# Keys of edge lists on GpSimd, and a norm's scalings split between ScalarE and VectorE, in a four-layer graph network

## The chip, the cores and the metric

The kernel runs on one core of a Trainium2 chip. The metric is the device time of the whole program in microseconds (us), shorter being better. Its inputs lie in HBM, and so does its output. Engines are named as the profile names them: PE is TensorE, DVE is VectorE, ACT is ScalarE, POOL is GpSimd, and SP is SyncE, whose queue carries most DMAs.

## The reference

The graph has 2048 nodes with 64 features each, in 8 batches. All batches share one symmetric adjacency matrix of int32, 2048 by 2048, with about 9 entries in a row, the diagonal among them. Four layers follow one another, each as `x = layernorm(x + layer(x, adj))`:

```
layer 0: h = layernorm(W(x*nw + nb + x)); softmax over the neighbours of leaky_relu(s1[i] + s2[j]); att @ h + h; elu
layer 1: f = softplus(x*w0 + b0); softmax over the neighbours, for each feature by itself; sum of the weights times f
layer 2: relu(x @ W_self + b_self + mean of the neighbours' x @ W_neigh + b_neigh); a layer norm of its own
layer 3: 4 heads of attention over neighbours with scores h.h; joined, leaky_relu, W_o; a fifth such attention; leaky_relu; layer norm
```

Layer 2 thus ends in two norms in a row: its own, with gain and shift, and then that of the sum `x + layer(x)`.

## The kernel before

Nodes are taken in 16 tiles of 128, one node to a partition. The tensor `X` holds the features of all nodes in SBUF through all layers, in fp32. The program is a row of stages, and each stage has pools of its own. "bufs=2" below means that a name has two buffers in turn, so that the third instance waits until the first has been read.

**The adjacency stage** (lines 296 to 383) makes two things out of the matrix: for tiles 0 to 8 a transposed copy of it for PE (`ET`, line 335), and for every tile a list of its edges. The loop goes over the 16 tiles, and a scheduler orders the instructions of every engine by their dependencies and priorities. For a tile:

- `at` (128 x 2048, int32, bufs=3) is loaded on SP's queue; `X` of the tile is loaded on ACT's queue.
- `key` (f16, bufs=2, line 327) is the number of the column, from 1, where there is an edge, and 0 elsewhere. One DVE instruction makes it from `at` and `node_no`.
- `on` (line 329) is the sign of it, by ACT, which adds up the degree `deg` at the same time. PE turns `on` over for the first nine tiles.
- Eight Max8 instructions on 256 columns each (line 338) give the largest keys of each segment in `tops`. Three rounds of Max8 and MatchReplace (lines 343 and 345) pick the 24 largest of those in order: the neighbours, `nbr`.
- `junk` (lines 347 and 349) counts the own edge and the list. A product on PE (line 354) gives every node its offset in the list of its group, `offs`; `ends` is the offset plus the degree.
- `nbrs` (line 359) holds four copies of a node's list, each kept in only one of the four groups of 32 nodes.
- `first_of` and `SelT` (lines 362 and 363) say which of the 384 places of a list belong to which node. PE multiplies `nbrs` by them (line 369) into `pl`; `at_`, `hit` and `src` (lines 373 to 380) turn `pl` into the row numbers that the gathers use later. `Sel` (line 371) is `SelT` turned over.
- After every second tile `node_products` makes layer 0's products and norm of two tiles; ACT squares at line 279, DVE adds up at 280, and `S1` at line 293 is its last instruction.

**Layer 0 and layer 1** follow. POOL issues layer 0's gathers of rows from `htab` in HBM (line 186), by `src`. Lines 539 to 548 belong to layer 1: there POOL casts `R` and subtracts (lines 544 and 548) beside DVE's `rest` (line 546).

**Layer 2** first makes products of every tile (lines 743 to 761, POOL's cast and subtraction at 754 and 760). In its main phase the order of PE, ACT, DVE and POOL is written out by hand, one step of PE after another: matrix products for tiles 0 to 8 (line 899), with the products over gathered rows for tiles 15 down to 9 (line 879) spread between them. `finish` (lines 844 and 845) makes a finished tile's sum with `S`, its ReLU, and takes its statistics. Tiles are put together in groups of the sizes `[1, 2, 3, 4, 3, 1, 1, 1]`; a full group becomes a `chain`, a Python generator of which `advance` takes a step or two after each step of PE:

- `newton` makes the factors of the first norm, by some twelve small DVE instructions.
- The first norm scales `S` into `z` in PSUM, one instruction to a batch (line 788 on ACT; in the last groups, where `shared` is true, every second one on DVE, line 786). `z` is multiplied by the gain (809) and added to `X` (810), and statistics are taken again.
- After `newton` once more, the second norm scales `X` in place, in the same manner.
- `show` copies the finished tile to `Xo` on POOL (line 828), and SP writes `Xo` to `xtab` in HBM by three DMAs (from line 829). The gathers of layer 3 read `xtab`.

POOL also issues the gathers of `ytab` in this order. `set_shifts` (lines 705 and 706), a part of layer 3's preparation, has PE wait for DVE once at step 104 of 144. `sides` (line 954) are layer 3's first products.

Of the kernel before, what the change touches and what calls it, by code (L numbers as in the profile page):

```python
# [21 lines left out]
F32 = mybir.dt.float32  # L22
# [5 lines left out]
AF = mybir.ActivationFunctionType  # L28
ALU = mybir.AluOpType
# [3 lines left out]
P = 128  # L33
# [15 lines left out]
def kernel(ctx: ExitStack, tc: tile.TileContext, ins: dict, out: bass.AP):  # L49
    nc = tc.nc  # L50
    x, adj = ins["x"], ins["adj"]
    B, N, D = x.shape
# [34 lines left out]
    def over(v, shape):  # L87

        for _ in shape[1:-1]:
            v = v.unsqueeze(1)  # L90
        return v.to_broadcast(shape)
# [70 lines left out]
    X = main.tile([P, NT, B, D], F32, name="X")  # L162
# [97 lines left out]
    def node_products(t0, wk, ps):  # L260
# [26 lines left out]
        for q, ph in enumerate(held):  # L287
# [8 lines left out]
    node_no = aw.tile([P, N], F16, name="node_no")  # L296
# [17 lines left out]
                                   op0=ALU.is_equal, op1=ALU.mult)  # L314
# [8 lines left out]
    for it in range(NT):  # L323
        at = ats.pop(it) if it in ats else load(it)
        nc.scalar.dma_start(X[:, it], x[:, it * P:(it + 1) * P, :].rearrange("b p d -> p b d"))
        key = ap_.tile([P, N], F16, name="key")
        nc.vector.scalar_tensor_tensor(key, at, 0, node_no, op0=ALU.is_gt, op1=ALU.mult)
        on = ap_.tile([P, N], BF16, name="on")
        nc.scalar.activation(on, key, AF.Sign, accum_out=deg[:, it:it + 1])
        for c in range(NCH if it < DENSE else 0):  # L330
            pt = aps.tile([P, TPC, P], F32, name="pt")
            for k in range(TPC):
                j0 = (c * TPC + k) * P
                nc.tensor.matmul(pt[:, k], on[:, j0:j0 + P], ident_bf, start=True, stop=True)
            nc.scalar.activation(ET[:, c * TPC:(c + 1) * TPC, it * P:(it + 1) * P], pt, AF.Copy, saturate=False)
        tops = ap_.tile([P, N // SEG, 8], F16, name="tops")
        for k in range(N // SEG):
            nc.vector.max(tops[:, k], key[:, k * SEG:(k + 1) * SEG])
        topf = tops.rearrange("p k m -> p (k m)")

        nbr = ap_.tile([P, SL + 1], F16, name="nbr")
        for k in range(0, SL, 8):
            nc.vector.max(nbr[:, k:k + 8], topf)
            if k + 8 < SL:
                nc.vector.match_replace(topf, nbr[:, k:k + 8], topf, 0.0)
        junk = ap_.tile([P, P], BF16, name="junk")
        nc.vector.scalar_tensor_tensor(junk, on[:, it * P:(it + 1) * P], 1.0, ident_bf, op0=ALU.mult, op1=ALU.mult,
                                       accum_out=own_edge[:, it:it + 1])
        nc.vector.scalar_tensor_tensor(junk[:, 0:SL], nbr[:, 0:SL], 0.0, nbr[:, 0:SL], op0=ALU.is_gt, op1=ALU.logical_and,
                                       accum_out=listed[:, it:it + 1])  # L350

        pl = aps.tile([P, 1 + GS * NG * (SL + 1)], F32, name="pl", bufs=1)
        poff = pl[:, 0:1]
        nc.tensor.matmul(poff, before, deg[:, it:it + 1], start=True, stop=True)
        nc.vector.tensor_scalar(offs[:, it:it + 1], poff, half0, 2.0 * GE, op0=ALU.add, op1=ALU.min)
        nc.vector.tensor_tensor(ends[:, it:it + 1], offs[:, it:it + 1], deg[:, it:it + 1], ALU.add)
        nc.vector.tensor_copy(nbr[:, SL:SL + 1], offs[:, it:it + 1])
        nbrs = ap_.tile([P, NG, SL + 1], F16, name="nbrs")
        nc.vector.tensor_tensor(nbrs, nbr.unsqueeze(1).to_broadcast(nbrs.shape),
                                group.unsqueeze(2).to_broadcast(nbrs.shape), ALU.mult)  # L360
        first_of = ap_.tile([P, GE], F16, name="first_of")
        nc.vector.tensor_scalar(first_of, node_no[:, 0:GE], offs[:, it:it + 1], None, op0=ALU.is_gt)
        nc.vector.scalar_tensor_tensor(SelT[:, it], node_no[:, 0:GE], ends[:, it:it + 1], first_of,
                                       op0=ALU.is_le, op1=ALU.mult, saturate=False)
        pl = pl[:, 1:].rearrange("p (g l) -> p g l", l=SL + 1)
        ps = aps.tile([P, GS, P], F32, name="ps", bufs=1)
        for s in range(GS):
            sel = SelT[:, it, s * P:(s + 1) * P]
            nc.tensor.matmul(pl[:, s * NG:(s + 1) * NG], sel, nbrs, start=True, stop=True)
            nc.tensor.matmul(ps[:, s], sel, ident_h, start=True, stop=True)  # L370
        nc.scalar.activation(Sel[:, it], ps, AF.Copy, saturate=False)
        at_ = ap_.tile([P, GS, NG], F32, name="at_")
        nc.vector.tensor_tensor(at_, place.unsqueeze(2).to_broadcast(at_.shape),
                                pl[:, :, SL].rearrange("p (s g) -> p s g", g=NG), ALU.subtract)
        hit = ap_.tile([P, GS * NG, SL], F32, name="hit")
        nc.vector.tensor_tensor(hit, node_no[:, 0:SL].unsqueeze(1).to_broadcast(hit.shape),
                                at_.rearrange("p s g -> p (s g)").unsqueeze(2).to_broadcast(hit.shape), ALU.subtract)
        nc.vector.scalar_tensor_tensor(hit, hit, 1.0, pl[:, :, 0:SL], op0=ALU.is_equal, op1=ALU.mult)
        nc.vector.tensor_reduce(at_.rearrange("p s g -> p (s g)"), hit, AX.X, ALU.add)
        nc.vector.tensor_scalar(src[:, it], at_, -1.0, 0.0, op0=ALU.add, op1=ALU.max)  # L380
        if it % HALF == HALF - 1:
            node_products(it - HALF + 1, ap_, aps)
# [9 lines left out]
    held, zs, stats = {}, {}, {}  # L392
# [319 lines left out]
    with ExitStack() as l2:  # L712
# [20 lines left out]
        S = wp.tile([P, NT, B, D], F32, name="S")  # L733
# [31 lines left out]
        pz = l2.enter_context(tc.tile_pool(name="l2pz", bufs=2, space=PSUM))  # L765
# [13 lines left out]
            for a in range(NP):  # L779
                nc.vector.bn_stats(st[:, k, a], v[:, 2 * a:2 * a + 2, :].rearrange("p b d -> p d b"))  # L780

        def scaled(to, v, stats, k, b, shared):
            rstd, nmr = stats
            own = slice(k * B + b, k * B + b + 1)
            if shared and b % 2:
                nc.vector.tensor_scalar(to[:, b], v[:, b], rstd[:, own], nmr[:, own], op0=ALU.mult, op1=ALU.add)
            else:
                nc.scalar.activation(to[:, b], v[:, b], AF.Identity, scale=rstd[:, own], bias=nmr[:, own])  # L788


        sizes = [1, 2, 3, 4, 3, 1, 1, 1]
        together, chains = [], []
        WAIT = 3

        def chain(ts, st):


            shared = len(sizes) < 2
            stats = newton(st)
            for _ in range(WAIT):  # L800
                yield False
            st = small.tile([P, 4, NP, 6], F32, name="l2_sx")[:, 0:len(ts)]
            for k, t in enumerate(ts):
                z = pz.tile([P, B, D], F32, name="z")
                for b in range(B):
                    scaled(z, S[:, t], stats, k, b, shared)
                    if b % 2:
                        yield True
                nc.vector.tensor_tensor(z, z, over(g2, [P, B, D]), ALU.mult)
                nc.vector.tensor_tensor(X[:, t], z, X[:, t], ALU.add)  # L810
                take_stats(st, k, X[:, t])
            stats = newton(st)
            for _ in range(WAIT):
                yield False
            for k, t in enumerate(ts):
                for b in range(B):
                    scaled(X[:, t], X[:, t], stats, k, b, shared)
                    if b % 2:
                        yield True
                    if b == 1 and k:  # L820
                        show(ts[k - 1])
            yield False
            show(ts[-1])
# [18 lines left out]
        def finish(it):  # L842
            sf = S[:, it].rearrange("p b d -> p (b d)")
            nc.vector.scalar_tensor_tensor(sf, sums.pop(it), r_deg[:, it:it + 1], sf, op0=ALU.mult, op1=ALU.add)
            nc.vector.tensor_scalar(sf, sf, 0.0, None, op0=ALU.max)
            if not together:
                together.append((small.tile([P, 4, NP, 6], F32, name="l2_st")[:, 0:sizes[0]], []))
            st, ts = together[0]
            take_stats(st, len(ts), S[:, it])
            ts.append(it)  # L850
            if len(ts) == sizes[0]:
                sizes.pop(0)
                together.pop()
                chains.append(chain(ts, st))

        by_list = list(range(NT - 1, DENSE - 1, -1))
        quads = [(it, s) for it in by_list for s in range(GS)]
# [78 lines left out]
    with early, ExitStack() as heads:  # L936
# [190 lines left out]
        with tc.manual_schedule(engines=engines):  # L1127
# [22 lines left out]
            t = NT - 1  # L1150
# [10 lines left out]
    with ExitStack() as fifth:  # L1161
# [17 lines left out]
        hss, pes, ws, wxs, zs, stats, sums = ({} for _ in range(7))  # L1179
# [116 lines left out]
        with tc.manual_schedule(engines=engines):  # L1296
# [5 lines left out]
            for u in range(len(units) + 7):  # L1302
# [19 lines left out]
                for plan, t0, t1 in ((after, 0, PAIRED - 2), (sooner, PAIRED - 2, PAIRED)):  # L1322
                    for j, fs in plan.items():
                        k = u - j - 2 * PER + 1
# [3 lines left out]
                for j, fs in alone.items():  # L1328
                    k = u - j - PER + 1
# [572 lines left out]
```

## Time and profile before

| | us |
|---|---|
| median of 3 runs | 2146.94 (2144.62 to 2149.81) |
| profiled execution, its own time | 2073.94 |
| profiled execution, its span | 2072.1 |
| mean granted TensorE clock of it | 0.802 |
| adjacency stage, from the start of the span | 0 to 209.9 |
| layer 2: products of every tile | 771 to 821 |
| layer 2: main phase, to the last matrix product | 821 to 975.2 |
| layer 2: the rest, to the last copy into `Xo` | 975.2 to 1015.0 |
| layer 3: heads | 1015 to 1650 |
| layer 3: fifth attention and last norm | 1650 to 2072.1 |

The span is what the profiler saw between the first and the last instruction. The profiled execution is 73.0 us shorter than the median of the runs; what is read in the profile is set against its own time. The page lists busy time of each engine first, then the span in 40 slices of 52 us with the busy share in tenths, then groups of instructions. A row of a group gives its line, its engine, its operation, what it writes and reads, and durations in ns. A row of a timeline gives start and length in us, and in square brackets how long the engine had been idle and whose work ended that.

### The profile page before, as it was taken

To read this page: it belongs to the slowest core of one execution; us is meant where nothing else is said; L and a number is where in the kernel's file an instruction comes from. 1 tells how busy PE (TensorE), PEld (TensorE's weight loads), DVE (VectorE), ACT (ScalarE), POOL (GpSimd) and SP (SyncE) were. 2 spreads that over 40 slices of the span, in tenths; PEclk is the share of its full clock that TensorE was granted. 3 is DMA by queue.
4 is the path that set the end of the run, shared out by engine and by line. 5 is a ranking of instruction groups with operands and counts; after the bars stand their busy time and mean duration, and the time that the engine had idled before them with its cause. 6 is when DMAs were issued, how large, how long until landed. Compare 5 with 4: busy or idle time off the path is not lost.

```text
span 2072.1 us, 35095 instructions
## 1 busy us (share of the span) xinstructions
PE 1559.9 (75%) x13062; PEld 897.8 (43%) x13062; DVE 1414.4 (68%) x3057; ACT 1024.7 (49%) x2504; POOL 1064.5 (51%) x993
## 2 busy tenths in 40 slices
PE   3573344542799987997299999999999689888873
PEld 3562121110333336332287788787787522222210
DVE  6879388886665556556555655656565489889986
ACT  4553134346822234347255545545455346777774
POOL 0000677761655526563245656556555287777760
PEclk9975555665999999998599999999999855555555
DMA  6421667660248842564233323333333165655541
GB/s 189 131 100 61 188 201 205 207 183 22 102 161 294 302 146 98 164 188 120 77 95 109 114 86 106 110 91 108 103 98 110 61 185 153 175 166 165 158 120 22
DMA packets 134242, 283.65 MB, mean 137 GB/s; under 512 B 64144, under 2 KB 66704, under 8 KB 131984
## 3 DMA queue, kind: packets, MB, share of 16 engines
q0 software_dynamic: 64896, 217.10, 34.9%
q1 hardware_dynamic: 52528, 60.03, 8.7%
q10 hardware_dynamic: 16640, 4.20, 0.9%
q8 instruction: 105, 1.72, 0.3%
q14 instruction: 73, 0.60, 0.1%
HBM read 245.35 MB, written 35.91 MB: 136 GB/s over the span
## 4 chain that ended last, share of the span: by engine, by line
PE 38%; DVE 10%; ACT 9%; POOL 6%; issue 6%; DMA 3%; SPq 0%; ACTq 0%; POOLq 0%; DVEq 0%
PE pscore L999 7%; PE pa L556 6%; PE po L1025 6%; PE pt L984 5%; POOL hs L186 4%; PE pm L954 3%; PE pm L1060 3%; PE pa L608 2%; PE po L1232 2%; PE pa L899 2%; ACT z L151 2%; DVE sc L1204 2%; ACT z L788 1%; PE py L748 1%; ACT wx L1215 1%
## 5 line engine op out<-in xcount | busy, mean ns | idle before, releaser
L186 POOL DMA_INDIRECT hs<-htab,src x192 | 183.7, 957 | 271.4 <-PE pe L408 209.0
L1008 DVE SCALAR_TENSOR_TENSOR w<-w,Sel 128x512 f32<-128x512 f32 (+1 forms) x192 | 188.9, 1010 | 174.7 <-ACT w L1002 174.1
L186 POOL DMA_INDIRECT xs<-xtab,src x192 | 221.0, 1151 | 67.8 <-issue 31.3
L556 PE MATMUL pa<-R,ET 128*128 128x512 bf16 x864 | 199.2, 388 | 50.9 <-POOL R L544 34.4
L186 POOL DMA_INDIRECT hs<-ktab,src x192 | 188.6, 982 | 53.7 <-issue 46.1
L999 PE MATMUL pscore<-U,xsT 64*128 64x64 f32 (+1 forms) x3072 | 205.1, 281 | 0.0
L1002 ACT ACTIVATE w<-pscore 128x1024 f32<-128x1024 f32 x128 | 130.9, 1023 | 138.4 <-PE pscore L999 131.3
L999 PEld LDWEIGHTS pscore<-U,xsT 64*128 64x128 f32 x3072 | 183.8, 190 | 21.7 <-issue 15.0
L986 ACT COPY xsT<-pt 128x512 f32<-128x512 f32 x192 | 112.1, 584 | 142.3 <-PE pt L984 140.5
L151 ACT ACTIVATE X<-X,ln_m,ln_r 128x64 f32<-128x64 f32 x256 | 87.2, 428 | 171.7 <-DVE ln_m L143 171.7
L1194 PE MATMUL pe<-hi,selTb 32*128 32x512 bf16 x576 | 134.4, 600 | 35.7 <-DVE pr L1199 35.2
L556 PEld LDWEIGHTS <-ET 128*128 128x128 fp8e4 x864 | 84.2, 99 | 174.0 <-issue 82.7
L1025 PE MATMUL po<-w,xs 128*64 128x64 f32 (+1 forms) x3072 | 143.7, 243 | 16.5 <-DVE o L1030 16.5
L1070 POOL TENSOR_TENSOR h<-h,h2h 128x512 f32<-128x512 f32 x45 | 57.1, 1269 | 166.2 <-DVE h2h L1066 165.9
L1025 PEld LDWEIGHTS po<-w,xs 128*64 128x64 f32 x3072 | 119.5, 137 | 43.9 <-DVE o L1030 18.8
L984 PE MATMUL pt<-ident,xs 128*128 128x128 f32 x768 | 128.1, 290 | 7.4 <-DMA xs<-xtab,src 6.1
L1215 ACT ACTIVATE wx<-hs,w 128x64 f32<-128x64 f32 x512 | 128.7, 340 | 0.1
L1199 DVE TENSOR_TENSOR pr<-pe,hs 128x1024 f32<-128x1024 f32 x96 | 116.8, 1217 | 16.6 <-DMA hs<-ktab,src 10.0
L1204 DVE TENSOR_REDUCE sc<-pr 128x16 f32<-128x1024 f32 x96 | 116.6, 1215 | 4.7 <-ACT w L1206 1.2
L186 POOL DMA_INDIRECT rs<-rtab,src x84 | 79.6, 948 | 71.9 <-PE pa L608 51.8
L565 DVE RECIPROCAL rec<-pa 128x256 f32<-128x256 f32 x32 | 54.1, 1729 | 78.0 <-PE pa L608 48.4
L428 DVE TENSOR_TENSOR hs<-hs,w 128x2048 f32<-128x2048 f32 x48 | 106.7, 2279 | 0.5 <-ACT w L418 0.5
(592 smaller groups left out, 3275.2 us busy)
## 6 DMA issues: line engine op xcount, KB each, us to landing
at<-in_adj SPq DMA_DIRECT2D x16, 1024.0 KB
rtab<-r SPq DMA_DIRECT2D x16, 512.0 KB
ptab<-hp SPq DMA_DIRECT2D x16, 384.0 KB
hi<-ptab SPq DMA_DIRECT2D x16, 384.0 KB
X<-in_x ACTq DMA_DIRECT2D x16, 256.0 KB
htab<-H SPq DMA_DIRECT2D x16, 256.0 KB
ytab<-y SPq DMA_DIRECT2D x16, 256.0 KB
ktab<-hb SPq DMA_DIRECT2D x16, 256.0 KB
```

Source lines behind the costliest of these rows:

```text
L151: nc.scalar.activation(v[:, b], v[:, b], AF.Identity, scale=rstd[:, k:k + 1], bias=nmr[:, k:k + 1])
L186: nc.gpsimd.indirect_dma_start(out=dst, out_offset=None, in_=table[:, :], in_offset=bass.IndirectOffsetOnAxis(ap=src[:, it, s, g:g + 1], a ...
L556: nc.tensor.matmul(po[h].rearrange("p a f -> p (a f)"), ET[:, jt, it * P:(it + 1) * P], R[:, jt, q, h].rearrange("p a f -> p (a f)"), star ...
L984: nc.tensor.transpose(pt[:, p], xss[k][n][:, p * P:(p + 1) * P], ident)
L999: nc.tensor.matmul(pscore[:, k_, f0:f0 + HN * ni].rearrange("p (h i) -> p h i", i=ni), xsTs[k][t][half, p], Us[it][half, p, :, i0:i0 + ni] ...
L1002: nc.scalar.activation(w.rearrange("p t k a h i -> p k t (a h i)"), pscore.rearrange("p k (t m) -> p k t m", t=n), AF.Exp)
L1008: nc.vector.scalar_tensor_tensor(wt, wt, 3.0e38, edge, op0=ALU.min, op1=ALU.mult)
L1025: nc.tensor.matmul(po[half, p, :, i0:i0 + ni], xss[k][t][:, f0:f0 + D], ws[k][:, t, k_, p], start=(s == 0 and p == 0), stop=(last and p == ...
L1194: nc.tensor.matmul(pe[:, k].rearrange("p b d -> p (b d)"), selTb[nodes, s * P:(s + 1) * P], hi[nodes, q], start=(q == 0), stop=(q == 2))
L1199: nc.vector.tensor_tensor(pr.rearrange("p k b d -> p (k b d)"), pes[u].rearrange("p k b d -> p (k b d)"), hss[u].rearrange("p k b d -> p ( ...
L1204: nc.vector.tensor_reduce(sc, pr, AX.X, ALU.add)
L1215: nc.scalar.activation(wxs[u][:, 0, b], hss[u][:, 0, b], AF.Copy, scale=ws[u][:, 0, b:b + 1])
```

## The change

There are two parts that have nothing to do with each other.

In the adjacency stage, the key of every tile is made by two POOL instructions, a comparison and then a product in place, and no longer by one DVE instruction. The copies `nbrs` of the lists are made by POOL too. Buffers stay as they are.

In layer 2, the second norm of every tile is made by `shared`: ACT scales four batches and DVE the other four. It was eight on ACT but for the last groups. The groups get the sizes `[1, 2, 3, 3, 3, 2, 1, 1]`. The last three groups (`late`, four tiles) make their first norm in the same way, in place in `S` in SBUF, and no longer in `z` in PSUM with ACT and DVE in turn.

```diff
@@ the adjacency stage @@
         key = ap_.tile([P, N], F16, name="key")
-        nc.vector.scalar_tensor_tensor(key, at, 0, node_no, op0=ALU.is_gt, op1=ALU.mult)
+        nc.gpsimd.tensor_scalar(key, at, 0, None, op0=ALU.is_gt)
+        nc.gpsimd.tensor_tensor(key, key, node_no, ALU.mult)
         on = ap_.tile([P, N], BF16, name="on")
...
         nbrs = ap_.tile([P, NG, SL + 1], F16, name="nbrs")
-        nc.vector.tensor_tensor(nbrs, nbr.unsqueeze(1).to_broadcast(nbrs.shape),
+        nc.gpsimd.tensor_tensor(nbrs, nbr.unsqueeze(1).to_broadcast(nbrs.shape),
                                 group.unsqueeze(2).to_broadcast(nbrs.shape), ALU.mult)
@@ layer 2 @@
-        def scaled(to, v, stats, k, b, shared):
+        def scaled(to, v, stats, k, b):
             rstd, nmr = stats
             own = slice(k * B + b, k * B + b + 1)
-            if shared and b % 2:
-                nc.vector.tensor_scalar(to[:, b], v[:, b], rstd[:, own], nmr[:, own], op0=ALU.mult, op1=ALU.add)
-            else:
-                nc.scalar.activation(to[:, b], v[:, b], AF.Identity, scale=rstd[:, own], bias=nmr[:, own])
-        sizes = [1, 2, 3, 4, 3, 1, 1, 1]
+            nc.scalar.activation(to[:, b], v[:, b], AF.Identity, scale=rstd[:, own], bias=nmr[:, own])
+        def shared(v, stats, k, b):
+            rstd, nmr = stats
+            for b_ in (b, b + 1):
+                scaled(v, v, stats, k, b_)
+            for b_ in (b + B // 2, b + B // 2 + 1):
+                own = slice(k * B + b_, k * B + b_ + 1)
+                nc.vector.tensor_scalar(v[:, b_], v[:, b_], rstd[:, own], nmr[:, own], op0=ALU.mult, op1=ALU.add)
+        sizes = [1, 2, 3, 3, 3, 2, 1, 1]
...
-        def chain(ts, st):
-            shared = len(sizes) < 2
+        def chain(ts, st, late):
             stats = newton(st)
...
             for k, t in enumerate(ts):
-                z = pz.tile([P, B, D], F32, name="z")
-                for b in range(B):
-                    scaled(z, S[:, t], stats, k, b, shared)
-                    if b % 2:
+                if late:
+                    z = S[:, t]
+                    for b in range(0, B // 2, 2):
+                        shared(z, stats, k, b)
                         yield True
+                else:
+                    z = pz.tile([P, B, D], F32, name="z")
+                    for b in range(B):
+                        scaled(z, S[:, t], stats, k, b)
+                        if b % 2:
+                            yield True
...
             for k, t in enumerate(ts):
-                for b in range(B):
-                    scaled(X[:, t], X[:, t], stats, k, b, shared)
-                    if b % 2:
-                        yield True
-                    if b == 1 and k:
+                for b in range(0, B // 2, 2):
+                    shared(X[:, t], stats, k, b)
+                    yield True
+                    if b == 0 and k:
                         show(ts[k - 1])
...
-                chains.append(chain(ts, st))
+                chains.append(chain(ts, st, len(sizes) < 3))
```

## The prediction

> **What bounds the kernel now.** I read the page's totals and slices first, since the change moves work between engines in two stages of one core, then each stage alone.
>
> ```profile
> PE 1559.9 (75%) x13062; PEld 897.8 (43%) x13062; DVE 1414.4 (68%) x3057; ACT 1024.7 (49%) x2504; POOL 1064.5 (51%) x993
> DVE  6879388886665556556555655656565489889986
> POOL 0000677761655526563245656556555287777760
> ```
>
> TensorE leads over the whole span, but the first four slices (0 to 207 us) are the stage that turns the adjacency into lists; there POOL is empty and DVE is busiest. Busy time by stretch (columns: length, PE, PEld, DVE, ACT, POOL with instruction counts, clock, DMA):
>
> ```profile
> 0.00:50.00 50.00, 18.46 (x112) 16.03 (x112) 31.80 (x149) 21.88 (x37) 3.24 (x12) 1.00 0.70 193
> 50.00:100.00 50.00, 28.93 (x171) 26.63 (x170) 41.99 (x166) 25.63 (x44) 0.00 (x0) 1.00 0.43 130
> 100.00:150.00 50.00, 34.55 (x196) 30.77 (x196) 36.83 (x136) 27.02 (x46) 0.00 (x0) 0.83 0.29 99
> 150.00:200.00 50.00, 18.61 (x108) 16.53 (x108) 50.00 (x199) 17.02 (x27) 0.00 (x0) 0.57 0.22 77
> ```
>
> DVE has 18, 8 and 13 us free in the first three and none in the last. So the late tiles are bound by DVE, the early ones by it in part: its waits from 15 to 155 us come to 29 us, 14.4 of them for ACT's squares (L279) and 9.1 for PE's list products (L369). The rows of the keys:
>
> ```profile
> L338 DVE MAX8 tops<-key x128: 404/420/428, 17.9 to 201.1; 128x8 f16<-128x256 f16 x128
> L327 DVE SCALAR_TENSOR_TENSOR key<-at,node_no x16: 2272/2282/2286, 15.3 to 195.3; 128x2048 f16<-128x2048 int32 x16
> L329 ACT ACTIVATE on<-key x16: 1892/1910/1913, 18.2 to 197.7; 128x2048 bf16<-128x2048 f16 x16
> ```
>
> From the first key to the last are 180.0 us for 15 tiles, 12.0 each. The last keys start at 154.56, 174.93 (two tiles on) and 195.3: 20.4 us a pair with DVE full, against 24 to 28 for most earlier pairs. Nothing of layer 0 runs ahead: POOL's first gather starts at 212.80, so a shift of this stage's end (209.9) moves everything after it.
>
> [...] L546 (`rest`, two SBUF inputs) takes 1.22 us alone; beside POOL's L548:
>
> ```profile
> 576.71 2.11 POOL L548 TENSOR_TENSOR R<-rest,R 128x1024 bf16<-128x1024 f32 x1
> 576.78 3.13 DVE L546 TENSOR_TENSOR rest<-r,R 128x1024 f32<-128x1024 f32 x1 [0.93 <-POOL R L544]
> ...
> 581.98 2.12 POOL L548 TENSOR_TENSOR R<-rest,R 128x1024 bf16<-128x1024 f32 x1
> 582.05 3.13 DVE L546 TENSOR_TENSOR rest<-r,R 128x1024 f32<-128x1024 f32 x1 [0.93 <-POOL R L544]
> ```
>
> It ends 1.08 us after POOL does, its own length: it ran only then. [...]
>
> **The change, part A: keys and list copies on POOL.**
> *Removed from DVE:* 16 keys of 2.28 and 16 `nbrs` of 0.26 us (L359 row): 40.6 us. A full pair falls from 20.4 to 20.4 − 4.56 − 0.52 = 15.3.
>
> *Added to POOL:* a compare (one input) and a product (two). The nearest rows:
>
> ```profile
> L754 POOL CAST Y<-y x16: 603/614/1072, 776.5 to 819.8; 128x512 bf16<-128x512 f32 x16
> L760 POOL TENSOR_TENSOR Y<-rest,Y x16: 1152/1158/1530, 781.1 to 821.9; 128x512 bf16<-128x512 f32 x16
> ```
>
> At 1024 elements the same forms take 1.03 (least of L544) and 2.12 (L548). So 0.81 and 1.88 ns an element with 0.2 fixed: 1.9 and 4.05 us at 2048. No row has a compare on int32. Lower bound 1.9[...]. I take 1.9 + 4.05 = 5.95, and 0.4 for `nbrs` (100 elements): 6.35 a tile, 12.7 a pair.
>
> *Do they overlap?* POOL was idle, so free cover would make this a gain. But much of what DVE keeps here reads two SBUF tensors or is a scalar operation on f16 (junk, ends, first_of, SelT, hit, the inverse root); the keys on POOL read SBUF throughout. The ones that pass freely are the eight Max8 a tile (3.4 us) and some reductions. Would Max8 cover the keys? Key has two buffers: POOL's compare for tile k+2 waits for the last Max8 of tile k. It starts just when DVE leaves the Max8 and comes to junk(k), two SBUF inputs, which waits out the compare; ends(k), a few short operations on, waits out the product. Then POOL makes nbrs(k), which was queued behind key(k+2); PE's products for tile k and DVE's `at_` wait for it. Only after that do Max8(k+1) end and POOL start again. I let about 0.8 us a tile overlap. Pair: 15.3 + 12.7 − 1.6 = 26.4 instead of 20.4.
>
> *Sum.* 15 tiles are 7.5 pairs. If the early pairs' waits stay beside the added 6.0: 7.5 × 6.0 = +45. If all their slack is used up: 7.5 × 26.4 − 180.0 = +18. The first key starts when its load lands (8.7) and not at 15.3, but takes 3.7 longer: −3. So +15 to +42. I take +34, near the upper end: the waits for PE's list products lie behind `nbrs`, which is now later, so that part doesn't shrink. ACT's Sign and the transposes shift with the key at no cost of their own. SP's adjacency loads have three buffers, freed by the compare: nothing. POOL's queue: the first gathers stand behind nbrs(15), long done by then: nothing.
>
> **Part B: layer 2.** Main phase 821 to 975, tail to 1016. Of the tail (the last tile):
>
> ```profile
> 1005.05 0.41 ACT L788 ACTIVATE z<-S,l_m,l_r 128x64 f32<-128x64 f32 x1 [0.84 <-DVE l_m L775]
> 1005.82 0.34 DVE L786 TENSOR_SCALAR z<-S,l_r,l_m 128x64 f32<-128x64 f32 x1
> ...
> 1008.67 0.70 DVE L809 TENSOR_TENSOR z<-z,g 128x512 f32<-128x512 f32 x1
> ...
> 1013.45 1.43 ACT L788 ACTIVATE X<-X,l_m,l_r 128x64 f32<-128x64 f32 x4 [5.20 <-DVE l_m L775]
> 1013.45 0.98 DVE L786 TENSOR_SCALAR X<-X,l_r,l_m 128x64 f32<-128x64 f32 x4
> ```
>
> In PSUM ACT and DVE take turns: 3.6 us. In SBUF, as in the second norm, four each run side by side in 1.4. So −2.2 for each of three such tiles, at most −6.6; the groupings move from 3,1,1,1 to 3,2,1,1, so the tiles bunch more at the end: I take −3. The last second norm was shared already: nothing. In the main phase 12 or 13 tiles give up four ACT operations (0.34 each) for four DVE ones (0.24): ACT −17 us, DVE +12. PE waits there only
>
> ```profile
> PE pa L879 <- DMA rs<-ytab,src: 11.6, 4, 5.9
> ```
>
> and once 2.1 us, so relief of ACT buys little. DVE's scalings are SBUF to SBUF in fp32[...]. `finish`, the stats and `set_shifts` (L706, for which PE waits) stand behind them on DVE. I take +5 (0 to +10). Layer 2: +2, range −7 to +7.
>
> **Sum:** 34 + 2 = +36: 2073.9 becomes about 2110 in a profiled execution. That execution is 73.0 us below the median of the runs; the difference is carried over as it is: 2146.9 + 36 = **2183 us**.
>
> **Rivals.**
> *No lock that counts, faster.* DVE's two-input operations slip in between POOL's instructions, or f16 runs quicker on POOL. Then full pairs fall from 20.4 to about 17, set by DVE's 15.3 with the wait for nbrs; the early ones stay: 2.5 full pairs × −3.4, and −3 at the start: −11. With layer 2's −3: −14, 2133. It decides where 2 × (key + 0.4) − 1.6 is less than the 5.1 us a pair saved: a key under 3.0 us. For it: POOL's emptiness. Against it: both price rows, and every L546 beside a POOL instruction.
> *Slow compare, slower still.* [...] Nothing in the trace excludes it.
> *Layer 2 pays more.* The tail's −6.6 with nothing lost ahead: 34 − 7 = +27, 2174.
>
> **How the numbers follow.** About 4 us (0.2%) is what a measurement of this kernel can tell from no change. Main case 0.50, slow compare 0.17, layer 2 paying 0.14: slower, 0.81. No lock: 0.19, of which 0.15 faster beyond 0.2% and 0.04 within. Range: from inside the no-lock case, 2140, to the slow compare with layer 2's loss[...], 2225.
>
> **What would show it.** POOL rows of about 1.9 and 4.05 us for the key; DVE's junk, ends, SelT and first_of lasting 2 to 4 us beside them; key to key 26 us a pair; the stage's last S1 (L293) near 244 and not 209.9; POOL some 100 us busy before it. In layer 2: 37 us, not 40, from the last matrix product to the last copy into `Xo`. I am wrong if DVE's two-input rows keep their lengths under POOL's keys, or if the pairs come in under 20 us.

## The result, and the profile after

Over four runs of each on one chip the changed kernel takes 2225.02 us (2214.34 to 2242.66), the kernel before 2148.38: a ratio of 1.0348 with a 95% interval of 1.0285 to 1.0411. It is slower, as forecast, but by 77 us and not by 36, and the median lies 0.02 us past the upper end of the range.

The profiled execution of the changed kernel took 2242.66 us, with a span of 2240.9. As a whole it can't be set against the profile of before, whose execution took 2073.94 us, some 75 us less than this program's runs here (see the last section). The adjacency stage can: here it ends at 265.2 at a mean granted clock of 0.65, and in `lists_only`, which has the same change of this stage, at 266.9 at 0.87.

Totals and slices of the changed kernel's page:

```profile
PE 1637.3 (73%) x13062; PEld 947.7 (42%) x13062; DVE 1508.6 (67%) x3081; ACT 1005.7 (45%) x2448; POOL 1205.5 (54%) x1041
DVE  8999748787565556556645555554554559899886
POOL 7666466664365544564234544554454357777761
```

POOL is now in every slice of the stage, and DVE, from which work was taken, is *busier* there than before. Busy time by stretch of the changed kernel (columns as before: length, PE, PEld, DVE, ACT, POOL, clock, DMA):

```profile
50.00:100.00 50.00, 27.94 (x166) 24.56 (x166) 49.04 (x125) 23.90 (x42) 32.07 (x11) 0.66 0.26 93
100.00:150.00 50.00, 24.57 (x159) 21.89 (x160) 46.92 (x120) 21.61 (x38) 29.30 (x9) 0.57 0.32 100
150.00:200.00 50.00, 28.03 (x136) 25.18 (x136) 48.68 (x129) 19.43 (x34) 29.35 (x9) 0.53 0.36 111
200.00:250.00 50.00, 11.79 (x62) 10.12 (x62) 49.72 (x135) 9.54 (x16) 29.30 (x9) 0.53 0.03 11
```

DVE is busy for 94% and more of each of these stretches, with 120 to 135 instructions in 50 us where the full stretch of before had 199: they are longer. The whole stage, once of before and once of after:

```profile
0.00:209.90 209.90, 101.78 (x592) 90.71 (x592) 170.19 (x693) 92.04 (x154) 3.24 (x12) 0.83 0.39 119
```

```profile
0.00:265.20 265.20, 103.80 (x592) 90.66 (x592) 247.67 (x661) 91.49 (x154) 159.59 (x60) 0.65 0.30 94
```

This is the account of it. DVE has 32 instructions fewer and 77.5 us more; its free time falls from 39.7 to 17.5. The difference, +55.3, is the longer stage. The sum over DVE's instructions of what each lasts beyond its usual length (the median of its line before) is 128 us, against 40.6 removed; the difference of 87 is more than 77.5 because DVE's instructions overlap (below, `ends` ends at 236.36 and the cast behind it starts at 236.28), which counts once in the busy time. The rows of the keys:

```profile
L339 DVE MAX8 tops<-key x128: 365/419/426, 27.6 to 256.1; 128x8 f16<-128x256 f16 x128
L327 POOL TENSOR_SCALAR key<-at x16: 5359/5360/5391, 6.1 to 232.7; 128x2048 f16<-128x2048 int32 x16
L328 POOL TENSOR_TENSOR key<-key,node_no x16: 4044/4047/4087, 11.6 to 238.2; 128x2048 f16<-128x2048 f16 x16
```

The product takes 4.05 us, as the prediction had it to the hundredth. The comparison takes 5.36, not 1.9. Where DVE's time goes is in the timeline of the changed kernel, here while POOL makes the last key:

```profile
232.71 5.36 POOL L327 TENSOR_SCALAR key<-at 128x2048 f16<-128x2048 int32 x1 [4.72 <-issue]
...
233.14 3.22 DVE L357 TENSOR_TENSOR ends<-offs,deg 128x1 f32<-128x1 f32 x1
...
236.48 1.71 DVE L363 TENSOR_SCALAR first_of<-node_no,offs 128x384 f16<-128x384 f16 x1
...
238.16 4.04 POOL L328 TENSOR_TENSOR key<-key,node_no 128x2048 f16<-128x2048 f16 x1
...
238.30 4.32 DVE L364 SCALAR_TENSOR_TENSOR SelT<-node_no,ends,first_of 128x384 fp8e4<-128x384 f16 x1
```

`ends` adds two columns of one element, 0.15 us before; here it lasts 3.22. SelT, 0.61 us before, ends 0.4 us after POOL's product, so hardly any of its work came earlier. The Max8 instructions, with one input, keep their 419 ns (420 before), also the seven that ran beside a key (0.36 to 0.42 us); a reduction of line 380 took 0.44 us beside a comparison and 0.44 alone.

This standing still of DVE while POOL reads SBUF, 3.9 us of SelT's 4.32 here, is what the prediction and the expectations call the lock. One thing differs from the prediction, in which two-input work waits out the comparison; the measurement decides. `ends`, with two inputs, is done at 236.36, 3.65 us after the comparison began and 1.7 us before it ended at 238.07; `first_of`, with one input, is done only at 238.19. In four other tiles it is the same: in one of them `ends` is done at 205.12, beside a comparison from 201.47 to 206.83. So the comparison held up `ends` for 3.65 of its 5.36 us, and `first_of` (1.71 us, 0.30 alone) to its end; the product held up SelT to its own end.

### The profile page after: what moved, and what is told of

Same layout as the page of the kernel before. It is cut to its first block, busy times and chain, and to the rows that moved or that the text cites. A ratio compares the mean times of both kernels' runs of the same rounds, so it can differ in the third digit from the quotient of the medians.

```text
span 2240.9 us, 35167 instructions
## 1 busy us (share of the span) xinstructions
PE 1637.3 (73%) x13062; PEld 947.7 (42%) x13062; DVE 1508.6 (67%) x3081; ACT 1005.7 (45%) x2448; POOL 1205.5 (54%) x1041
## 4 chain that ended last, share of the span: by engine, by line
PE 36%; DVE 12%; ACT 8%; issue 6%; POOL 5%; DMA 3%; another core or an unknown queue 1%; SPq 0%; ACTq 0%; POOLq 0%; DVEq 0%
PE pscore L1010 7%; PE po L1036 6%; PE pa L557 6%; PE pt L995 5%; POOL hs L186 3%; PE pm L1071 3%; PE pm L965 3%; PE pa L609 2%; DVE sc L1215 2%; DMA hs<-ktab,src 1%; DVE pr L1210 1%; PE po L1243 1%; ACT z L786 1%; ACT wx L1226 1%; PE py L749 1%
## 5 line engine op out<-in xcount | busy, mean ns | idle before, releaser
L186 POOL DMA_INDIRECT xs<-xtab,src x192 | 211.6, 1102 | 77.1 <-issue 39.5
L1010 PE MATMUL pscore<-U,xsT 64*128 64x64 f32 (+1 forms) x3072 | 231.1, 293 | 13.7 <-issue 10.1
L1010 PEld LDWEIGHTS pscore<-U,xsT 64*128 64x128 f32 x3072 | 203.0, 200 | 41.2 <-issue 29.9
L1036 PE MATMUL po<-w,xs 128*64 128x64 f32 (+1 forms) x3072 | 164.9, 255 | 15.5 <-DVE o L1041 12.4
L1036 PEld LDWEIGHTS po<-w,xs 128*64 128x64 f32 x3072 | 132.0, 145 | 52.0 <-issue 29.9
L995 PE MATMUL pt<-ident,xs 128*128 128x128 f32 x768 | 140.1, 310 | 16.2 <-DMA xs<-xtab,src 9.5
L327 POOL TENSOR_SCALAR key<-at 128x2048 f16<-128x2048 int32 x16 | 85.8, 5362 | 73.3 <-issue 37.3
L995 PEld LDWEIGHTS pt<-ident,xs 128*128 128x128 f32 x768 | 89.8, 153 | 45.2 <-issue 14.4
```

Of the source, the lines that this page charges most:

```text
L186: nc.gpsimd.indirect_dma_start(out=dst, out_offset=None, in_=table[:, :], in_offset=bass.IndirectOffsetOnAxis(ap=src[:, it, s, g:g + 1], a ...
L995: nc.tensor.transpose(pt[:, p], xss[k][n][:, p * P:(p + 1) * P], ident)
L1010: nc.tensor.matmul(pscore[:, k_, f0:f0 + HN * ni].rearrange("p (h i) -> p h i", i=ni), xsTs[k][t][half, p], Us[it][half, p, :, i0:i0 + ni] ...
L1036: nc.tensor.matmul(po[half, p, :, i0:i0 + ni], xss[k][t][:, f0:f0 + D], ws[k][:, t, k_, p], start=(s == 0 and p == 0), stop=(last and p == ...
```

## The experiments

Each ran beside the kernel before on one chip. The first series is `lists_only`, `layer2_only`, `copies_only` and `prices`; the second is `after_again`, `cast_key` and the two `lock` kernels; the third is the rest. On the chips of the first and third series the kernel before takes 2067 and 2069 us, on that of the second 2160; so differences and ratios are compared, not times.

An end of the stage is read from one execution. `layer2_only` has the stage of before, with the same order of instructions on DVE, ACT and PE, and there it ends at 203.1, not at 209.9. A difference against 209.9 is therefore known to some 7 us only.

### The parts by themselves, and the price of a comparison

`lists_only` has the adjacency stage's part of the change, `layer2_only` the other part, `copies_only` only the second of these two edits:

```diff
-        nc.vector.scalar_tensor_tensor(key, at, 0, node_no, op0=ALU.is_gt, op1=ALU.mult)
+        nc.gpsimd.tensor_scalar(key, at, 0, None, op0=ALU.is_gt)
+        nc.gpsimd.tensor_tensor(key, key, node_no, ALU.mult)
...
-        nc.vector.tensor_tensor(nbrs, nbr.unsqueeze(1).to_broadcast(nbrs.shape),
+        nc.gpsimd.tensor_tensor(nbrs, nbr.unsqueeze(1).to_broadcast(nbrs.shape),
```

> Only the adjacency stage of the change (keys and list copies on POOL); layer 2 as before. Theory 1 (the lock between POOL's keys and DVE's two-input work, with a comparison that takes 5.4 us and not 1.9): the stage ends near 265 us instead of 210, and the whole program is 65 to 80 us slower, nearly all of what the change costs. Theory 2 (a good part is lost in layer 2): 45 to 55 us slower, no more than the stage itself. Theory 3 (layer 0 behind the stage is slowed too, by a cause of its own): its gathers span 271 us instead of 245 here as well, and the total is near 80.

> Only layer 2 of the change; the adjacency stage as before. Theory 1: between 2 us faster and 8 us slower than before, the tail a little shorter, the main phase longer by waits of PE for DVE. Theory 2: 20 us slower or more. Layer 0 as before under both; if its gathers span 271 us here too, Theory 3 is wrong in blaming the adjacency stage.

> Only the list copies (nbrs) on POOL; the key stays on DVE, layer 2 as before. Theory 1: POOL runs 0.38 us a tile with nothing ahead of it, so hardly any DVE instruction is blocked; DVE saves 0.26 us a tile, and the stage ends within 3 us of before: 4 us faster to 2 us slower. Theory 3 in the form 'any work of POOL in the stage disturbs layer 0': some 25 us slower.

| kernel | median, us | before, us | ratio (95%) | difference |
|---|---|---|---|---|
| lists_only | 2123.94 | 2066.51 | 1.0279 (1.0254 to 1.0305) | +57.4 |
| layer2_only | 2067.97 | 2066.51 | 1.0006 (0.9996 to 1.0016) | +1.5 |
| copies_only | 2064.88 | 2066.51 | 0.9993 (0.9982 to 1.0005) | −1.6 |

The stage ends at 266.9 in lists_only, and layer 0's gathers span 244 us as before. So the keys on POOL are nearly the whole cost; layer 2 and the list copies can't be told from nothing. That is between theories 1 and 2: less than the 65 us of the one, a little more than the 55 of the other. It is what the stage itself lost (266.9 − 209.9 = 57.0), and layer 2 has no part in it.

`prices` adds eleven POOL instructions of 128x2048 to one tile of the kernel before; it ran once, to read their lengths:

> The kernel before with eleven POOL instructions of 128x2048 added once, in tile 3, to read their lengths; the results aren't used. If the comparison is slow because its input is int32, is_gt, copy and product on int32 all take about 5.4 us and the same on f16 or f32 1.9. If comparing is what is slow, is_gt takes 5.4 on f32 and f16 too, and the copy of int32 1.9. Copy f16 1.9, product of two f16 4.05, iota 1.83.

The rows of this kernel for what they write, `trial`:

```profile
L331 POOL TENSOR_SCALAR trial<-at x1: 5392/5392/5392, 23.5 to 23.5; 128x2048 f16<-128x2048 int32 x1
L332 POOL CAST trial<-at x1: 1883/1883/1883, 31.6 to 31.6; 128x2048 f16<-128x2048 int32 x1
...
L335 POOL TENSOR_SCALAR trial<-node_no x1: 5359/5359/5359, 39.0 to 39.0; 128x2048 f16<-128x2048 f16 x1
L336 POOL TENSOR_SCALAR trial<-trial_f x1: 5373/5373/5373, 44.5 to 44.5; 128x2048 f16<-128x2048 f32 x1
...
L339 POOL COPY trial<-node_no x1: 1905/1905/1905, 60.3 to 60.3; 128x2048 f16<-128x2048 f16 x1
L340 POOL TENSOR_TENSOR trial<-node_no x1: 3690/3690/3690, 62.3 to 62.3; 128x2048 f16<-128x2048 f16 x1
```

Neither expectation holds: it is not int32 (the cast of it takes 1.88), and not comparing (L336 multiplies by a number, and takes as long). Each of the five `tensor_scalar` on POOL, `is_gt` or `mult`, took 5.36 to 5.39 us, from int32, f32 and f16 alike; a copy or cast to f16 takes about 1.9. I had priced a `tensor_scalar` by a cast because both have one input.

### The lock, apart from the dependencies

Three POOL instructions are put ahead of DVE's key in the kernel before; DVE overwrites what they write. They are copies in one kernel and iotas in the other, which wait for and release the same things.

```diff
+        for _ in range(3):
+            nc.gpsimd.tensor_copy(key, node_no)                       # lock_copies
+            nc.gpsimd.iota(key, pattern=[[1, N]], base=1, ...)        # lock_iotas
         nc.vector.scalar_tensor_tensor(key, at, 0, node_no, op0=ALU.is_gt, op1=ALU.mult)
```

> The kernel before with three POOL copies (128x2048 f16, 1.9 us each, 5.7 together) into the key's buffer ahead of DVE's key in each tile; what they write is overwritten by it. They read SBUF. Theory 1 (the lock): DVE's two-input instructions are blocked by nearly as much as POOL runs; 40 to 70 us slower. Rival (the key on POOL costs time by its place in the chain of dependencies, not by a lock): within 10 us of lock_iotas.

> The same with three iotas of 1.84 us (5.5 together), which write SBUF and read nothing; all dependencies are those of lock_copies. Theory 1: two-input instructions of DVE keep their lengths[...]; 2 us faster to 12 us slower than before. Rival: as slow as lock_copies.

Against 2160.34 us, lock_copies takes 2225.68 (1.0306, 1.0267 to 1.0344) and lock_iotas 2169.17 (1.0029, 0.9996 to 1.0062). The last S1 starts at 263.0 and at 210.6; it was 209.9 before. Rows of `first_of` and `SelT`, first with copies, then with iotas:

```profile
L364 DVE TENSOR_SCALAR first_of<-node_no,offs x16: 294/1121/1940, 29.9 to 255.4; 128x384 f16<-128x384 f16 x16
L365 DVE SCALAR_TENSOR_TENSOR SelT<-node_no,ends,first_of x16: 596/1370/2137, 32.0 to 255.8; 128x384 fp8e4<-128x384 f16 x16
```

```profile
L364 DVE TENSOR_SCALAR first_of<-node_no,offs x16: 304/1088/1262, 27.6 to 203.0; 128x384 f16<-128x384 f16 x16
L365 DVE SCALAR_TENSOR_TENSOR SelT<-node_no,ends,first_of x16: 597/602/606, 28.9 to 203.4; 128x384 fp8e4<-128x384 f16 x16
```

5.7 us of POOL a tile that reads SBUF cost 53 us of the stage; 5.5 us that only writes cost 0.7 us of it, and the program's +9 us can't be told from nothing. With iotas SelT is never blocked (0.60 us, 0.61 before), and `first_of` is (1.09 us, 0.30 before); with copies both are. Why `first_of` is, no run here shows. The rival, that the place in the chain of dependencies costs the time, falls for 5.5 us of POOL a tile; for the 9.4 us of the changed key it was not tried apart from the lock.

### The whole change again, and the key at the price that was predicted

`after_again` is the changed kernel itself. `cast_key` is lists_only with a cast in place of the comparison, so that the key costs what the prediction took, 1.9 + 4.05 us:

```diff
-        nc.gpsimd.tensor_scalar(key, at, 0, None, op0=ALU.is_gt)
+        nc.gpsimd.tensor_copy(key, at)
         nc.gpsimd.tensor_tensor(key, key, node_no, ALU.mult)
```

> The changed kernel as it is, beside the kernel before on this chip, because the parts alone sum to about +59 us here (57.4 and 1.5) and the first comparison, where both kernels were slower, gave +77. Theory 1 (the parts add up): 52 to 66 us slower, and layer 0's gathers span 245 us as before. Theory 3 (the whole change slows layer 0 as well): 75 to 90 us slower, and the gathers span 271 us.

> As lists_only, but POOL makes the 0 and 1 by a copy of at into f16 instead of the comparison (the adjacency holds only 0 and 1; the comparison is left out). By the measured prices this key costs 1.9 + 4.05, which is what the prediction took. If the prediction's way of adding was right and only the price was wrong, the stage ends near 244 and the program is 28 to 40 us slower than before. If the structure of the sum was wrong too (more overlap than taken), it is 5 to 22 us slower; if the lock is of no matter, it is faster.

> The same as cast_key (copy instead of comparison). There the stage lengthened by 21 us and the program by 50, because the clock fell more often in layer 3's heads than for other kernels of that chip. If this belongs to the chip, then on one whose clock stays up in the heads the program is 17 to 28 us slower than before; if the kernel itself makes the heads slower, 45 to 55 us here too.

after_again: 2225.20 against 2160.34, +65 (1.0276, 1.0239 to 1.0314). Its gathers span 272 us, as theory 3 had it; but on that chip they do so in lock_iotas too (213.5 to 485.4), which changes nothing behind the stage. So theory 3 falls: that is the chip's, not the change's.

cast_key came to +50 on that chip (1.0225, 1.0201 to 1.025), with a stage that ended at 230.8. The stage fits the smaller of the two sums expected, the program lies above both. Most of the rest lay in layer 3's heads, from the first gather of `xtab` to the last write of `ktab`: 704 us where lock_iotas has 674 on that chip, at mean clocks of the whole runs of 0.75 to 0.76 and 0.765 to 0.775. cast_key_2, the same kernel on the third series' chip, at a mean clock of 0.78 to 0.79, gives 2090.04 against 2068.94: +21.1 (1.0099, 1.0079 to 1.0118), with the stage's end at 231.3, +21.4. Its stage, its keys and DVE's wait for ACT's squares:

```profile
0.00:231.30 231.30, 105.50 (x592) 93.65 (x592) 205.97 (x661) 90.94 (x154) 104.61 (x60) 0.64 0.35 108
L327 POOL CAST key<-at x16: 1889/1890/1906, 6.0 to 201.8; 128x2048 f16<-128x2048 int32 x16
DVE h_v L280 <- ACT sq L279: 1.0, 1, 1.0
```

### A third buffer, and a version without POOL

`three_keys` gives the key of lists_only three buffers. `sign_first` takes the key's work off DVE in another way: ACT's Sign, which was made from the key, is made from `at`, and the key from the Sign. It rests on an adjacency without negative entries: one, which is no edge in the kernel before, would be −1 in `on` and in the degree. `sign_layer2` adds layer 2's part of the change.

```diff
-        key = ap_.tile([P, N], F16, name="key")
+        key = ap_.tile([P, N], F16, name="key", bufs=3)                          # three_keys
```

```diff
-        nc.vector.scalar_tensor_tensor(key, at, 0, node_no, op0=ALU.is_gt, op1=ALU.mult)
-        nc.scalar.activation(on, key, AF.Sign, accum_out=deg[:, it:it + 1])
+        nc.scalar.activation(on, at, AF.Sign, accum_out=deg[:, it:it + 1])       # sign_first
+        nc.vector.tensor_tensor(key, on, node_no, ALU.mult)
```

> As lists_only, with three buffers for the key instead of two, so that POOL needn't wait for the last Max8 of tile k before key k+2. If the lock alone decides, DVE is blocked by as much as POOL runs against its two-input work, whenever that is: 45 to 60 us slower than before. If the prediction's point was right that the two buffers put the key just onto DVE's locked work and Max8 could have covered it, 10 to 40 us slower.

> The kernel before, but ACT takes its Sign straight from at (0 and 1 in the adjacency, int32), and DVE makes the key as the product of on and node_no, two 2-byte inputs. Nothing goes to POOL. If DVE does this product in well under the 2.28 us of the old key, the stage, bound by DVE, gets shorter: 5 to 18 us faster. If it takes as long, or the wait for ACT counts, within 5 us of before.

> sign_first with layer 2 of the change as well. Layer 2 measured 1.0006 (0.9996 to 1.0016) alone, so this is within 3 us of sign_first.

Against 2068.94 us: three_keys 2123.16 (1.0263, 1.0246 to 1.028), +54 where two buffers gave +57. POOL does get ahead (its last key starts at 223.1, in lists_only at 234.4), and still hardly anything is won: the buffer isn't what decides. sign_first takes 2046.88 us (0.989, 0.9873 to 0.9908), 22 us faster than before, and so beats both kernels; sign_layer2 2050.18 (0.9915, 0.9898 to 0.9931), which is 3.3 us more where within 3 was expected, and no better. The row of sign_first's key:

```profile
L329 DVE TENSOR_TENSOR key<-on,node_no x16: 1206/1218/1222, 16.9 to 171.7; 128x2048 f16<-128x2048 bf16 x16
```

1.22 us instead of 2.28, 17 us in 16 tiles, and the stage ends at 185.2 instead of 209.9; what goes beyond 17 us there is no more than the 7 us by which that end is uncertain.

## Why the prediction was right or wrong, step by step

**The lock: right.** It was the reason for the forecast of slower, and lock_copies against lock_iotas shows it by itself. Where it was told too simply is that two-input work waits out the whole comparison: `ends` waited for 3.65 of its 5.36 us. That POOL stood empty was no evidence that its work is free.

**The comparison's price: this is the term that failed.** In the 5.95 us of the key, 1.9 for the comparison was read from a cast; `tensor_scalar` took 5.36, and the key 9.4. The upper end of the range took a slower comparison, which no row showed; the measurement shows that the operation isn't even the point (5.37 us for a product with a number). What 3.46 us a tile are worth: lists_only less cast_key_2, 57.4 − 21.1 = 36 us. On the second series' chip the stage says nearly the same, 265.1 of after_again less 230.8 of cast_key, 34 us; the medians of the two differ by only 14.5, cast_key's heads being 10 us longer and the rest open. The rival "slow compare" named the right place.

**The pair of tiles: nearly right.** At the price taken a pair with DVE full was 26.4 us. In cast_key_2 the mean over the 15 steps from 6.0 to 201.8 is 2 × 13.05 = 26.1, but so close a fit is luck: from a key to the second one after it there are 20 to 22 us for the first four, and 26.2 to 30.2, on average 27.9, for the ten others.

**The choice within +15 to +42: wrong.** I took +34, since the waits of the early tiles would stay. Those for PE's list products did, 7.5 us in cast_key_2 where there were 9.1, as the prediction argued; those for ACT's squares went, from 14.4 to 1.0, and DVE's free time in the stage fell from 39.7 to 25.3. And the sum had hardly a term for what stands behind the last key: the last key is started while DVE still has the tile before it to do, and from there to the last S1 there are 29.5 us, not 14.6; the sum had 3.7 for it. In cast_key_2 the keys lie 15.8 us further apart in all (+37 was taken), the first starts 9.3 earlier (6.6 was taken), and 14.9 come behind the last: +21.4. So the stage was set 13 us too high at its own price, and 36 too low for the price: 34 − 13 + 36 = 57, which is lists_only.

**That two key buffers place the key on DVE's blocked work: so it runs, but it hardly matters.** The comparison starts just behind the last Max8, as told (232.71, the Max8 ends at 232.56). With three buffers 3 us come back, which the intervals don't tell from none. Max8 lasts 3.4 us a tile against 9.4 of POOL, and DVE's order is fixed: its instructions lose 114 us in that stage by lasting longer, 125 in lists_only.

**Removed work, `nbrs`, queues: right.** copies_only at −1.6 us has no cost that can be told.

**Layer 2: +2 forecast, +1.5 measured (−0.8 to +3.3, from the interval times 2066.5), by smaller terms.** In layer2_only the main phase lasts 153.9 us as before (154.0; +5 was forecast, an estimate), and from its end to the last copy into `Xo` there are 38.6 us where there were 39.8 (−3 was forecast). The equal length of the main phase hides a cost: PE was busy for 138.8 us there at a mean clock of 0.96, before for 142.2 at 0.93, and its waits rose from 13.7 to 17.2 us. The stretch and the waits:

```profile
814.80:968.70 153.90, 138.80 (x629) 50.71 (x630) 100.86 (x361) 58.01 (x151) 89.29 (x97) 0.96 0.55 163
PE pm L705 <- DVE pm L701: 7.3, 1, 7.3
PE pa L889 <- DMA rs<-ytab,src: 4.7, 7, 1.4
PE pa L889 <- DVE l_t L126: 3.1, 1, 3.1
PE pa L909 <- DVE rest L758: 2.1, 1, 2.1
```

`set_shifts` does make PE wait for DVE, as predicted, for 7.3 us, and DVE is late once more, for 3.1; the waits for gathered rows, 11.6 before, fell to 4.7. From the busy times and the waits I estimate 3 us for the main phase at an equal clock; one execution of each doesn't show so little for certain. The late first norms did shrink from 3.6 to 1.44 us:

```profile
999.01 1.44 ACT L785 ACTIVATE S<-S,l_m,l_r 128x64 f32<-128x64 f32 x4 [4.36 <-DVE l_m L775]
999.02 0.98 DVE L794 TENSOR_SCALAR S<-S,l_r,l_m 128x64 f32<-128x64 f32 x4
```

**From the profiled execution to the median: not the same sum on every chip.** The parts add to +59 on the first series' chip, on which the whole change was not run. On the second series' chip, where the kernel before ran at a mean clock of 0.770 to 0.785 (0.785 to 0.805 on the first's), it gave +65, and in the first comparison, where the changed kernel ran at 0.753 to 0.775, +77; their intervals overlap. So 59 of the 77 us are told by the terms above. Where the other 18 come from stays open; part may be the heads, below: on the second series' chip after_again spends 694 us in them and lock_iotas 674.

## What to carry to other kernels

An empty engine is a poor place for the busy one's long instructions where its reading holds the busy one up, as POOL's did DVE here: 91 us of copies, 5.7 a tile, cost the stage 53 us. Count what the busy engine keeps that is held up (here SelT, 4.32 us instead of 0.61, `ends` and `first_of`) and what is not (Max8). Price an instruction by a row of the same operation; that two have one input each doesn't make them alike (5.36 us against 1.9 here), and a price that no row shows deserves a wide bound. Before moving work, look whether it can be made cheaper where it is (here by ACT's Sign, which needed only another input: 1.22 us a key instead of 2.28).

## What the runs showed of the hardware that was not expected

POOL's `tensor_scalar` took 5.36 us on 128x2048, from f16, f32 and int32 and for comparing and multiplying alike: slower than its product of two tensors (3.69 to 4.84 us) and 2.8 times a copy. DVE's `ends` was free again 3.65 us after it began, `first_of` only at its end.

The same kernel differs by some 4% between chips: before takes 2067, 2069, 2148 and 2160 us. The page's rows of the granted clock, of lists_only on the first series' chip and of the changed kernel on the slower one of the first comparison, show one likely reason:

```profile
PEclk9998556665599999999679999999999955555555
```

```profile
PEclk9655555555699999999589989988998965555555
```

In layer 3's heads (slices 21 to 31, the slice that counts as first being 0) the clock holds at 9 tenths and more on one, and drops to 0.50 on the other, from 1209 us on for 3 to 11 us at a time every 40 to 48 us. The length of the heads differs between kernels and runs: they last 622 us in lists_only, 694 and 708 in two executions of the changed kernel, 674 in lock_iotas. The clock doesn't account for all of it: its mean in the heads is 0.99 in lists_only and 0.90 where they last 708, and 622 × 0.99 / 0.90 = 684 is an estimate from these figures. Layer 0's gathers, 272 us on the slower chip against 244, go with the chip too; why, no run here settles.
